# A graph-network kernel: its prologue rewritten in groups of two tiles, the lowest bf16 part made through PSUM

## The chip, the core and the metric

One core of one Trainium2 chip runs the whole program. The time is the device time of one execution in microseconds (us); of several executions the median is given. A profiled execution gives in addition a record of each instruction, from which the views in this document are taken. The engines are called TensorE (PE), VectorE (DVE), ScalarE (ACT), GpSimd (POOL) and SyncE (SP); SP here only issues DMAs.

## The reference

```python
h = jnp.maximum(_layernorm(x, axis=-1), 0.0)      # x: (6250, 256) f32
deg = segment_sum(ones, edge_dst)                 # 100000 edges, dst sorted
h = sage_mean(h, ...)      # h @ W1_self + mean of h over in-edges @ W1_neigh + b1
h = sage_pool(h, ...)      # relu(h @ W2_pool + b2_pool), max over in-edges, two products
h = sage_gcn(h, ...)       # (sum over in-edges + h) / (deg + 1) @ W3_neigh + b3
h = sage_mean(h, ...)      # W4_self, W4_neigh, b4
out = x + (h @ W_fc + b_fc)
```

Each edge adds row `h[src]` into node `dst`. The destinations crowd at the low nodes (they are 6250 times the square of a uniform number), so the first node tiles have very many edges and the last have few.

## The kernel before

The 6250 nodes are 49 tiles of 128. Precision is kept by writing each f32 value as a sum of three bf16 parts (`hi`, `mid`, `lo`), which TensorE multiplies with 0/1 or count matrices exactly and adds up in PSUM.

**Prologue (L648 to L967).** It makes three things. First, the table of layer 1: x is loaded tile by tile, normalized, put through relu, split into the three parts in the SBUF tensor `Z1`, and stored to `tab_h` in DRAM. `layer_norm` (L684) does five tiles at a time: per tile `bn_stats` and `bn_aggr` on VectorE, then for the group a square root (ScalarE), a reciprocal and a bias (VectorE), five relu activations (ScalarE), the cast `hi` (ScalarE, L701), the subtraction of `hi` (VectorE, L702), the cast `mid` (GpSimd, L703), the subtraction that gives `lo` (VectorE, L704) and one store of five tiles (SP, L705). x has three buffers of five tiles; group g + 3 is loaded behind group g. Second, the edge lists are put in place: `dst` and `src` are transposed by TensorE (`turn`, L856), the first edge of each window of nodes is found (`begins`, `begin_nodes`, `row_begins`), windows of edges are gathered by GpSimd and transposed (`window_rows`, L818), and keys are made of them (`window_keys`, `tail_keys`). `tail_keys` also makes the 0/1 table `M` (L894) and three checks of the input (L872, L901, L912), whose results are only read at the end of the kernel. Third, products of the weights (`product`) are made, one step per group.

Beside these the prologue begins the first count matrix: `made` (L646) is a list of 139 matrix steps for node block 0, each of which makes two one-hot tiles (`hs` by two ScalarE instructions or one on VectorE, L326 to L333; `hm` on VectorE, L335) and multiplies them (L341). `made.advance(part0)` does 62 of the 139 here (45 per cent).

**Layer 1 (L970 to L1032).** Node blocks 8 and up get their rows by gathers: GpSimd issues 474 indirect DMAs of 128 rows each (L478), one-hot tiles of the keys are made on VectorE (L474), TensorE adds the three parts (L500), VectorE adds the sums into `acc` with `M` (L529). The ring of gathered rows holds 14. The eight low blocks are dense products of count matrices with `Z1` (L559). All matrix steps that are left, and the dense products, form the hub, which is spread evenly over the gathers (L507), except for the last 24. Per gather one step of each "aside" generator is taken as well; `segments` (L591) is the only one. It loads `src` and `dst` once more, in blocks, for layer 2.

The order of the instructions on each engine is not that of the code. A planner lays them out by its own costs; a DMA with `keep_in_program_order`, and an engine inside `manual_schedule`, keep the order of the code. An instruction waits on its engine's queue in order, and everything behind it waits too, DMA issues on SP, ScalarE and GpSimd among them. DMAs of SP and ScalarE take eight completion semaphores in turn; one that takes a semaphore waits until the DMA that had it before has landed.

Of the kernel before, what the change touches and what calls it, by code (L numbers as in the profile page):

```python
# [27 lines left out]
PART0 = 45  # L28
# [50 lines left out]
def fast_path(  # L79
# [511 lines left out]
    def segments():  # L591
# [3 lines left out]
        for b, tb in enumerate(BLOCKS):  # L595
            t0 = offs[b] // P
            for flat, put in ((sflat, srcI), (dflat, dstI)):
                nc.sync.dma_start(
                    put[:, t0 : t0 + tb],
                    flat[offs[b] : offs[b + 1]].rearrange("(p t) -> p t", t=tb),  # L600
                )
# [43 lines left out]
    part0 = sum(k_of[:WT]) * PART0 // 100  # L645
    made = Hub(build(0, As[0], (sk1, mk1, 0), bpool, psb1, part0))  # L646

    with ExitStack() as pro:  # L648
        pst = pro.enter_context(tc.tile_pool(name="pst0", bufs=3, space=PSUM))
        psm = pro.enter_context(tc.tile_pool(name="psm0", bufs=3, space=PSUM))  # L650
        ep = pro.enter_context(tc.tile_pool(name="turn", bufs=1))


        dstI = scratch(T, I32)
        nc.sync.dma_start(dstI, dflat[0:EP].rearrange("(p t) -> p t", t=T))
# [6 lines left out]


        lp = pro.enter_context(tc.tile_pool(name="fln", bufs=2))
        xts = []
        groups = [(i0, min(5, NT - i0)) for i0 in range(0, NT, 5)]

        def load_x(g):
            i0, n = groups[g]
            xt = lp.tile([P, 5, FI], F32, name="xt", bufs=3)[:, :n, :]  # L670
            nf = min(n, NFULL - i0)
            if nf < n:
                nc.vector.memset(xt[(NREM // 32) * 32 :, nf, :], 0.0)
                nc.sync.dma_start(xt[:NREM, nf, :], x[NFULL * P : N, :])
            nc.sync.dma_start(
                xt[:, :nf, :],
                x[i0 * P : (i0 + nf) * P, :].rearrange("(c p) f -> p c f", p=P),
            )
            xts.append(xt)

        for g in range(3):
            load_x(g)

        def layer_norm(g):  # L684
            i0, LG = groups[g]
            xt = xts[g]
            mv = lp.tile([P, 5, 2], F32, name="mv")[:, :LG, :]
            for c in range(LG):
                st = lp.tile([P, 6], F32, name="st", bufs=4)
                nc.vector.bn_stats(st, xt[:, c, :])  # L690
                nc.vector.bn_aggr(mv[:, c, :], st)
            sd, rs, nb = (lp.tile([P, 5], F32, name=v)[:, :LG] for v in ("sd", "rs", "nb"))
            nc.vector.tensor_scalar(sd, mv[:, :, 1], EPS, None, op0=ALU.add)
            nc.scalar.activation(sd, sd, AF.Sqrt)
            nc.vector.reciprocal(rs, sd)
# [4 lines left out]
            hi, mid, lo = (Z1[:, i0 : i0 + LG, i * FI : (i + 1) * FI] for i in range(3))  # L700
            nc.scalar.copy(hi, xt)  # L701
            nc.vector.tensor_sub(xt, xt, hi)  # L702
            nc.gpsimd.tensor_copy(mid, xt)  # L703
            nc.vector.tensor_sub(lo, xt, mid)  # L704
# [25 lines left out]
        select(0)  # L730


# [9 lines left out]
        dlast = ep.tile([P, 1], F32, name="dlastf")  # L742
        nc.vector.tensor_copy(dlast, dstI[:, T - 1 : T])
        under = ep.tile([P, NC * P], BF16, name="under")
        nc.vector.tensor_scalar(under, iota_n, dlast, None, op0=ALU.is_gt)
        pc = bank(psm, "pm", "pc_c", (NC,))
        for c in range(NC):
            nc.tensor.matmul(pc[:, c : c + 1], under[:, c * P : (c + 1) * P], ones_b,
                             start=True, stop=True)
        cF = ep.tile([P, NC], F32, name="cF")  # L750
        nc.vector.tensor_scalar(cF, pc, float(P - 1), None, op0=ALU.min)
        cI = ep.tile([P, NC], I32, name="cI")
        nc.vector.tensor_copy(cI, cF)
# [5 lines left out]
        def begins(c):  # L759
            if c in (1, 2):  # L760
                row = As[0].rearrange("p s n -> p (s n)").bitcast(I32)[:, (c - 1) * T : c * T]
            else:
                row = ep.tile([P, T], I32, name="drow", bufs=1)
# [17 lines left out]
        def row_begins(b0, b1, cs):  # L781
            pa = bank(psm, "pm", "pa", (RB, 2))
            for b in range(b0, b1):
                for c in cs:
# [3 lines left out]
                                 start=False, stop=True)  # L788
            nc.vector.tensor_copy(atF[:, b0:b1, :], pa[:, b0:b1, :])
# [28 lines left out]
        def window_rows(b):  # L818
            mk = mk1 if b < RB1 // P else mkR
            got = []  # L820
            for flat in (dflat, sflat):
                t = ep.tile([P, P], I32, name="wrow", bufs=4)
# [4 lines left out]
                got.append(t)  # L827
            f = ep.tile([P, 2, P], F32, name="wrowf", bufs=2)
# [3 lines left out]
            for i in range(2):  # L832
                nc.tensor.transpose(pt[:, i, :], f[:, i, :], ident)
            r = b * P if b < RB1 // P else b * P - RB1
# [21 lines left out]
        def turn():  # L856
            for r, put in ((rD[:, JC:, :], dT), (rS, srcT)):
                for c0 in range(0, JR - JC, 4):
                    n = min(4, JR - JC - c0)
                    rF = ep.tile([P, 4, P], F32, name="rF", bufs=2)  # L860
                    nc.vector.tensor_copy(rF[:, :n, :], r[:, c0 : c0 + n, :])
                    pt = bank(pst, "pt", "pt_e", (4, P))
                    for c in range(n):
                        nc.tensor.transpose(pt[:, c, :], rF[:, c, :], ident)
                    nc.vector.tensor_copy(
                        put[:, c0 * P : (c0 + n) * P],
                        pt[:, :n, :].rearrange("p a b -> p (a b)"),
                    )
# [1332 lines left out]
```

## Time and profile before

| | us |
|---|---|
| median of 3 runs | 2768.62 (2766.17 to 2773.96) |
| the profiled execution | 2777.43 |
| its span, first to last instruction | 2775.6 |
| prologue, up to the first gather of layer 1 | 130.5 |
| layer 1, up to the last product of its gathers | 134.0 to 747.4 |

The profile's lines name the source line, the engine, the operation and the tiles (output `<-` inputs). A time in brackets behind an instruction is the idle time ahead of it, with what ended it. In a table of stages each engine has its busy time and, in brackets, its count of instructions. The profile follows one execution, and times of it are compared only with that execution's own.

### The profile page before, as it was taken

Reading aid. Unit: us, or ns where it says so; the run is one execution under the profiler, and the core shown is the slowest. Engines: PE = TensorE matmul, PEld = TensorE weight load, DVE = VectorE, ACT = ScalarE, POOL = GpSimd, SP = SyncE. Lnnn points to the kernel's source line nnn. Section 1 sums busy time; section 2 is a strip of 40 time slices with the busy share of each in tenths; the row PEclk is TensorE's granted clock in tenths of the full one; section 3 lists DMA queues with packets and bytes.
Section 4 is the critical chain, followed back from the end, with each engine's and each line's share of the span. In section 5 each row is a group of like instructions: output and inputs, shape, how many; then the busy total and the mean of one; then the engine's idle time right before and its main releaser. Section 6 shows DMA issues by size and latency. Waiting matters only on the chain.

```text
span 2775.6 us, 39285 instructions
## 1 busy us (share of the span) xinstructions
PE 2382.4 (86%) x11671; PEld 1280.7 (46%) x11671; DVE 2074.6 (75%) x5484; ACT 912.3 (33%) x2202; POOL 1940.8 (70%) x2260
## 2 busy tenths in 40 slices
PE   4379999999978566798899978985999999999998
PEld 2136666666544222343344433442444444565554
DVE  7978676766489889889899997871667776466655
ACT  3668676764268778421311121110000011000000
POOL 4277777777467777777777777754777776677775
PEclk9589999999989687899999988998999999999999
DMA  6556777777699999999999999977999998888886
GB/s 207 175 151 193 207 209 209 220 230 226 182 342 362 330 350 356 353 360 344 335 353 356 355 356 332 339 271 279 378 378 385 382 371 321 262 242 241 238 243 198
DMA packets 350539, 806.43 MB, mean 291 GB/s; under 512 B 55806, under 2 KB 147430, under 8 KB 350284
## 3 DMA queue, kind: packets, MB, share of 16 engines
q0 software_dynamic: 146160, 514.05, 56.6%
q1 hardware_dynamic: 137576, 207.04, 20.5%
q10 hardware_dynamic: 66580, 82.73, 8.9%
q8 instruction: 94, 1.54, 0.2%
q14 instruction: 129, 1.06, 0.1%
HBM read 605.25 MB, written 199.17 MB: 290 GB/s over the span
## 4 chain that ended last, share of the span: by engine, by line
PE 51%; DMA 27%; DVE 11%; issue 5%; POOL 3%; ACT 1%; SPq 0%; DVEq 0%; POOLq 0%; ACTq 0%
PE pd L559 14%; DMA X<-rows,srcIf 11%; PE pg L500 11%; PE pd L551 5%; DMA ring<-tab_h,srcT 4%; DVE run L1342 3%; DMA ring<-tab_s,srcE 3%; PE pm_hp L1010 3%; PE pm_hp L1013 3%; PE pm_prf L1269 3%; DMA rows<-X 3%; PE pd L552 2%; DVE X L1342 2%; POOL X L1361 2%; PE pg L495 2%
## 5 line engine op out<-in xcount | busy, mean ns | idle before, releaser
L1361 POOL DMA_INDIRECT X<-rows,srcIf x782 | 744.6, 952 | 281.4 <-issue 144.5
L1342 DVE SCALAR_TENSOR_TENSOR run<-run,samef,X 128x512 f32<-128x512 f32 x758 | 571.3, 754 | 52.5 <-DMA X<-rows,srcIf 48.4
L500 PE MATMUL pg<-ring,hot 128*128 128x259 bf16 (+1 forms) x2448 | 514.0, 321 | 59.7 <-DMA ring<-tab_h,srcT 34.6
L478 POOL DMA_INDIRECT ring<-tab_h,srcT x474 | 456.3, 963 | 152.2 <-issue 54.0
L529 DVE SCALAR_TENSOR_TENSOR acc<-pg,M,acc 128x256 f32<-128x256 f32 (+2 forms) x694 | 357.0, 539 | 107.6 <-PE pg L500 80.5
L478 POOL DMA_INDIRECT ring<-tab_r,srcE x342 | 334.1, 977 | 130.3 <-issue 56.9
L559 PE MATMUL pd<-r,ae 128*128 128x512 bf16 x1536 | 373.5, 384 | 35.4 <-DVE acc L1127 35.3
L478 POOL DMA_INDIRECT ring<-tab_s,srcE x314 | 300.1, 956 | 114.5 <-PE pg L496 36.2
L500 PEld LDWEIGHTS <-hot 128*128 128x128 bf16 x2448 | 240.3, 99 | 274.5 <-issue 113.3
L1342 DVE SCALAR_TENSOR_TENSOR X<-X,samef,run 128x512 f32<-128x512 f32 x379 | 281.6, 743 | 41.3 <-DVE hm L369 8.6
L551 PE MATMUL pd<-zt,ac 128*128 128x512 bf16 x882 | 305.0, 380 | 5.6 <-DMA ac<-tab_a 4.0
L559 PEld LDWEIGHTS <-ae 128*128 128x128 fp8e4 x1536 | 151.3, 99 | 251.9 <-issue 106.5
L474 DVE TENSOR_SCALAR hot<-iota_bf,keyE 128x128 bf16<-128x128 bf16 x656 | 160.3, 268 | 108.6 <-PE pg L500 78.3
L552 PE MATMUL pd<-zt,ac 128*128 128x256 bf16 x882 | 241.0, 273 | 0.2 <-DVE zt L307 0.2
L559 PE MATMUL pd<-zt,ac 128*128 128x512 bf16 x816 | 224.7, 380 | 0.0
L1269 PE MATMUL pm_prf<-unf,hTf 128*128 128x512 f32 x392 | 189.9, 612 | 4.6 <-ACT hTf L1259 4.6
L341 PE MATMUL pb<-hm,hs 128*128 128x392 bf16 x461 | 150.9, 349 | 48.6 <-DVE hm L335 43.0
L333 ACT ACTIVATE hs<-ht,onef 128x128 bf16<-128x128 bf16 x423 | 161.7, 393 | 85.5 <-PE pb L341 84.5
L559 PE MATMUL pd<-Z,A 128*128 128x256 bf16 (+1 forms) x1176 | 185.6, 273 | 0.4 <-ACT A L346 0.2
L474 DVE TENSOR_SCALAR hot<-iota_bf,keyT 128x128 bf16<-128x128 bf16 x474 | 122.8, 270 | 61.2 <-PE pg L500 59.2
L335 DVE TENSOR_SCALAR hm<-iota_w,mk 128x392 bf16<-128x392 f16 x461 | 151.6, 339 | 17.3 <-PE pb L341 16.3
L332 ACT ACTIVATE ht<-iota_bf,sk 128x128 bf16<-128x128 bf16 x423 | 159.0, 396 | 7.0
(342 smaller groups left out, 3457.6 us busy)
## 6 DMA issues: line engine op xcount, KB each, us to landing
rows<-X SPq DMA_DIRECT2D x385, 256.0 KB
tab_r<-r ACTq DMA_DIRECT2D x49, 384.0 KB
tab_t<-th SPq DMA_DIRECT2D x49, 256.0 KB
rows<-hpf SPq DMA_DIRECT2D x49, 256.0 KB
th<-tab_t ACTq DMA_DIRECT2D x49, 256.0 KB
X<-rows,srcIf POOLq DMA_INDIRECT x782
ac<-tab_a ACTq DMA_DIRECT2D x90, 112.0 KB
tab_h<-Z SPq DMA_DIRECT2D x9, 965.0 KB
```

Source lines behind the costliest of these rows:

```text
L332: nc.scalar.activation(t, iota_b, AF.Abs, bias=sk[:, r : r + 1])
L333: nc.scalar.activation(hots[0], t, AF.Relu, bias=one, scale=-1.0)
L474: nc.vector.tensor_scalar(hot[j], iota_b, keyT[:, j - jb : j - jb + 1], None, op0=ALU.is_equal)
L478: nc.gpsimd.indirect_dma_start(out=ring[:, j % deep, :], out_offset=None, in_=table, in_offset=bass.IndirectOffsetOnAxis(ap=srcT[:, j - jb ...
L500: nc.tensor.matmul(pg[:, : F + c], hot[j], X[:, part * F : (part + 1) * F + c], start=(k == 0 and part == 2), stop=(k == n - 1 and part == 1),
L529: nc.vector.scalar_tensor_tensor(acc[d], half, m, acc[d], op0=ALU.mult, op1=ALU.add)
L551: nc.tensor.matmul(hold[0], a, z[:, : 2 * F], start=(s == ss[0]), stop=False)
L552: nc.tensor.matmul(hold[0][:, :F], a, z[:, 2 * F :], start=False, stop=(s == ss[-1]))
L559: nc.tensor.matmul(hold[0][:, : F + c], a, z[:, part * F : (part + 1) * F + c], start=(s == ss[0] and part == 2 and s != own), stop=(s == ...
L1269: nc.tensor.matmul(pm, hT[:, c, :], un[:, c, :], start=False, stop=(c == KH - 1))
L1342: nc.vector.scalar_tensor_tensor(put, held, st, row, op0=ALU.mult, op1=ALU.max)
L1361: nc.gpsimd.indirect_dma_start(out=X[:, k, :], out_offset=None, in_=tab_p, in_offset=bass.IndirectOffsetOnAxis(ap=srcI[:, t : t + 1], axis=0),
```

## The change

- Groups have two tiles instead of five (25 groups); x has seven buffers of two tiles instead of three of five. `layer_norm` is cut into pieces, `stats`, `inverse`, `scaled`, `middle` and `lowest`, and the pieces of neighbouring groups are interleaved: in iteration g come the reciprocal of g + 1, the statistics of g + 2 with the relus and the cast of g + 1 among them, the closing of g - 1, the load of g + 6 and the subtraction of g. VectorE keeps this order (`manual_schedule`).
- The lowest part is no longer subtracted on VectorE. TensorE multiplies the rest by the identity into PSUM (f32) and adds the middle part times minus the identity (bf16); ScalarE copies the difference from PSUM as bf16.
- All other work of the prologue (`extras`) is laid in pieces behind the subtractions of the groups 2, 6, 8, 10, 13, 15, 17 and all from 18 on, with a piece that needs another engine's answer one or more groups behind the piece that asked. The first statistics come before any of it.
- The three checks of the input go to layer 1 as the first aside generator (`tail_checks`), ahead of `segments`; the loads of `segments` keep their place in the code instead of being drawn into the start of the prologue.
- `part0` is 10 instead of 62: ten matrix steps of block 0 are done in the prologue and 129 left to the hub.
- Gathers of windows have eight buffers instead of four; rows for `begins` are put into tensors that exist already.

```diff
-PART0 = 45
...
-    part0 = sum(k_of[:WT]) * PART0 // 100
+    part0 = 10
...
-        groups = [(i0, min(5, NT - i0)) for i0 in range(0, NT, 5)]
+        groups = [(i0, min(2, NT - i0)) for i0 in range(0, NT, 2)]
...
-            xt = lp.tile([P, 5, FI], F32, name="xt", bufs=3)[:, :n, :]
+            xt = lp.tile([P, 2, FI], F32, name="xt", bufs=7)[:, :n, :]
...
-            nc.scalar.copy(hi, xt)
-            nc.vector.tensor_sub(xt, xt, hi)
-            nc.gpsimd.tensor_copy(mid, xt)
-            nc.vector.tensor_sub(lo, xt, mid)
+        def middle(g):
+            i0, LG = groups[g]
+            nc.vector.tensor_sub(xts[g], xts[g], Z1[:, i0 : i0 + LG, :FI])
+            nc.gpsimd.tensor_copy(Z1[:, i0 : i0 + LG, FI : 2 * FI], xts[g])
+            pl = lows[g] = bank(psl, "pl", "pl", (2, FI))[:, :LG, :]
+            nc.tensor.matmul(pl, ident, xts[g], start=True, stop=False)
+
+        def lowest(g):
+            i0, LG = groups[g]
+            pl = lows.pop(g)
+            nc.tensor.matmul(pl, minus_b, Z1[:, i0 : i0 + LG, FI : 2 * FI], start=False, stop=True)
+            nc.scalar.copy(Z1[:, i0 : i0 + LG, 2 * FI : 3 * FI], pl)
             nc.sync.dma_start(
                 tab_h[i0 * P : (i0 + LG) * P, :].rearrange("(c p) f -> p c f", p=P),
                 Z1[:, i0 : i0 + LG, :],
...
+        with tc.manual_schedule(engines={mybir.EngineType.DVE}):
+            stats(0)
+            select(0)
+            inverse(0)
+            stats(1, lambda: scaled(0))
+            chunks_at()
+            for c in range(NC):
+                begins(c)
+            for g in range(len(groups)):
+                if g + 1 < len(groups):
+                    inverse(g + 1)
+                if g + 2 < len(groups):
+                    stats(g + 2, lambda: scaled(g + 1), lambda: lowest(g - 1) if g else None)
+                else:
+                    if g + 1 < len(groups):
+                        scaled(g + 1)
+                    lowest(g - 1)
+                if g + 7 - 1 < len(groups) and g:
+                    load_x(g + 7 - 1)
+                middle(g)
+                next(steps, None)
+                if g in (2, 6, 8, 10, 13, 15, 17):
+                    extras((2, 6, 8, 10, 13, 15, 17).index(g))
+                elif g > 17:
+                    extras(g - 17 + 6)
+            lowest(len(groups) - 1)
+            for _ in steps:
+                pass
+            tail_keys()
...
-             aside=[segments()])
+             aside=[tail_checks(wk), segments()])
```

In `extras` the parts from group 6 on are those of the old code, in this order: the first node rows and the first halves of the transposed lists (2, 6), the window gathers of the first block, eight in a row (8), the other node rows (10), the transposed windows (13, 15, 17) and the keys of block 0 (17), then the narrower windows with `check_room` (18, 21) and the tile numbers (23), with one or two of the ten matrix steps in each of the groups 18 to 24.

More of the change, by code (lines that the diff above doesn't have):

```diff
@@ L685, in layer_norm, with inverse, scaled @@
+        def inverse(g):
+            mv, sd = norms.pop(g)
+            rs = lp.tile([P, 2], F32, name="rs", bufs=3)[:, : groups[g][1]]
+            nc.vector.reciprocal(rs, sd)
+            norms[g] = mv, rs
+        def scaled(g):
             i0, LG = groups[g]
             xt = xts[g]
[L687 to L691, printed above, removed]
@@ L762, in begins @@
             else:
-                row = ep.tile([P, T], I32, name="drow", bufs=1)
+                row = same.bitcast(I32) if c else srcI
             nc.gpsimd.indirect_dma_start(
```

261 lines of the change are left out of this document (163 added, 98 removed).

## The prediction

> **What bounds it now.** I read the span in stages first. The columns are busy time and instruction count of each engine, the granted TensorE clock, the DMA share and rate.
>
> ```profile
> core 0: us, PE busy (x) PEld busy (x) DVE busy (x) ACT busy (x) POOL busy (x), PEclk, DMA share, GB/s
> 8.00:50.00 42.00, 16.62 (x65) 12.58 (x66) 29.40 (x96) 12.39 (x25) 22.52 (x55) 1.00 0.66 205
> 50.00:125.00 75.00, 30.72 (x94) 12.87 (x92) 70.73 (x225) 47.72 (x109) 14.84 (x71) 0.67 0.61 192
> 125.00:130.50 5.50, 2.78 (x8) 1.15 (x9) 5.50 (x15) 5.02 (x18) 2.98 (x106) 0.50 0.42 147
> 130.50:225.00 94.50, 71.21 (x372) 39.22 (x371) 77.83 (x341) 67.08 (x209) 70.42 (x70) 0.87 0.59 162
> 225.00:450.00 225.00, 204.46 (x1405) 142.94 (x1404) 159.17 (x610) 155.32 (x425) 170.63 (x179) 0.99 0.72 205
> 450.00:700.00 250.00, 248.94 (x1696) 174.67 (x1694) 173.50 (x648) 153.83 (x394) 189.64 (x199) 1.00 0.75 220
> ```
>
> The prologue is VectorE's: 70.73 of 75 us busy from 50 to 125. Before 50 VectorE idles 12.6 of 42 us. The rest of layer 1 has two masters: GpSimd issues one gather per 225/179 = 1.257 us, and from 450 TensorE is full too (248.94 of 250). The first stretch is worse: 70 gathers in 94.5 us, where 70 x 1.257 = 88 would do, so 6.5 us are lost there. From layer 2 on the instruction order of the changed program is the same on every engine; the whole change is therefore the move of the end of layer 1.
>
> Where the prologue ends is read from GpSimd's timeline: the last middle part, the 164 memsets of `lim`, then a wait for the last stored rows, then the first gather.
>
> ```profile
> 122.21 1.07 POOL L703 CAST Z<-xt 128x1024 bf16<-128x1024 f32 x1 [3.64 <-DVE xt L702]
> 123.23 4.75 POOL L967 MEMSET lim<- 1x1 f32 x164
> 130.52 1.03 POOL L478 DMA_INDIRECT ring<-tab_h,srcT  x1 [2.54 <-PE pb L341]
> ```
>
> **Start of the new prologue.** Two rows say why the old one starts late: VectorE waits 3.85 us for the shifted copy of dst, and ScalarE issues the first weight loads at 22.97.
>
> ```profile
> 18.26 1.09 DVE L872 TENSOR_TENSOR wrongf<-X,X 128x896 bf16<-128x896 int32 x1 [3.85 <-DMA X<-dflat]
> ```
> ```profile
> 22.97 0.84 ACTq L261 DMA_DIRECT2D wl<-in_L_gnn_W_self  x2
> 28.20 2.56 ACT L698 ACTIVATE xt<-xt,nb,rs 128x256 f32<-128x256 f32 x5 [13.64 <-DVE nb L696]
> 30.67 0.19 ACT L694 ACTIVATE sd<-sd 128x5 f32<-128x5 f32 x1
> 30.79 1.26 ACT L701 CAST Z<-xt 128x1280 bf16<-128x1280 f32 x1
> ...
> 46.71 0.59 ACT L266 COPY wT<-pt_w 128x512 f32<-128x512 f32 x1 [3.01 <-PE pt_w L265]
> ```
>
> In the changed program the first weight load stands on ScalarE's queue ahead of the first normalization and shares a completion semaphore with that copy of dst, which is there at 18.26; the second stands behind the first normalization. So ScalarE cannot begin before about 18.5, and 0.8 of issue, two tiles of 2.56/5 = 0.51, a square root and a cast of 1.26 x 2/5 = 0.50 put group 0's subtraction, the first of all, at about 21.5. The old first cast ends at 32.05; the new one, at 20.8, is some 11 us ahead, since the statistics no longer queue on VectorE with the work on dst.
>
> **VectorE's work after that.** Groups of VectorE's instructions, 0 to 130.5 (count | busy us, mean ns | idle before):
>
> ```profile
> L690 DVE BATCH_NORM_STATS2 st<-xt 128x6 f32<-128x256 f32 x49 | 18.8, 399 | 0.8 <-DMA xt<-in_x 0.8
> L702 DVE TENSOR_TENSOR xt<-xt,Z 128x1280 f32<-128x1280 f32 (+1 forms) x10 | 14.6, 1459 | 0.8 <-ACT Z L701 0.8
> L704 DVE TENSOR_TENSOR Z<-xt,Z 128x1280 bf16<-128x1280 f32 (+1 forms) x10 | 14.5, 1448 | 0.0
> L335 DVE TENSOR_SCALAR hm<-iota_w,mk 128x392 bf16<-128x392 f16 x34 | 13.5, 440 | 0.0
> ...
> L894 DVE TENSOR_SCALAR M<-tile_of 128x6 f32<-128x6 f32 (+6 forms) x41 | 4.0, 167 | 0.0
> ...
> L693 DVE TENSOR_SCALAR sd<-mv 128x5 f32<-128x5 f32 (+1 forms) x10 | 1.7, 168 | 0.0
> L912 DVE SCALAR_TENSOR_TENSOR wrongf<-wrongf,X 128x640 bf16<-128x640 bf16 x1 | 1.6, 1610 | 0.0
> L901 DVE TENSOR_TENSOR wrongf<-X,dB 128x128 bf16<-128x128 f32 x5 | 1.3, 278 | 0.0
> ...
> L844 DVE TENSOR_TENSOR mk<-mk,sk 128x512 f32<-128x512 f32 x1 | 0.7, 679 | 0.0
> ```
>
> From 8 to 130.5 VectorE is busy 29.4 + 70.7 + 5.5 = 105.6 us. Out go the lowest part, 14.5; the checks L872, L901, L912, 4.0, with their reduction of about L872's length, 1.1 (an estimate); 24 of 34 one-hots at 0.440, 10.6; and `M`, 4.0, which now stands behind the last subtraction. In come 24.5 subtractions of 0.679 for 14.6, +2.0, and three small instructions in 25 groups instead of 10, 15 x 3 x 0.168 = 7.6. That leaves 81; about 5 are done before 21.5 (three groups' statistics, 6 x 0.399, one selection, small ones) and 4 are keys behind the last subtraction: **72 us** after 21.5.
>
> **ScalarE beside it.** A group's loop, when the square root is queued last: reciprocal 0.17, statistics 0.40, bias 0.17, two tiles 1.02, lowest copy from PSUM 0.59 (L266's row), cast 0.50, root 0.19, in all 3.0; with the root first 2.0. The order has both. VectorE's own loop is about 2.3 by single durations, 1.9 as they overlap. In the 11 iterations with no side work I charge 0.8 each: 9 us (bounds 0 and 2.0 each). In the other 14 the side work covers it.
>
> **GpSimd in between.** Eight window gathers in a row, then four, stand ahead of the next group's middle cast; TensorE's closing product, ScalarE's copy, and in order behind it casts and roots wait for that.
>
> ```profile
> 29.50 0.95 POOL L823 DMA_INDIRECT wrow<-dflat,atI  x1 [0.30 <-issue]
> ```
>
> At 1.25 each the eight take 10 us, while VectorE has some 8 us of its own until it needs the next root, and the copies behind add 2.5: 4.5 us lost; the four cost 2.5. Together 7 (0 to 13).
>
> **TensorE's new product** is not a term while the clock is up: two records of 0.59 for a 512-wide f32 product, and a bf16 one of less, are under 2 of some 3.5 us a group.
>
> ```profile
> L277 PE MATMUL pm_b<-w2pf,b1c 128*128 128x512 f32 x8 | 3.6, 592 | 0.0
> ```
>
> The last subtraction ends near 21.5 + 72 + 9 + 7 = 109.5; a small cast and then the 4.75 of `lim`, now not hidden behind a store of four tiles, give the first gather at about 115.5, against 130.5: **15 us earlier**. DMA is no term: its share was 0.61 of 75 us with the same bytes, and six groups are loaded ahead.
>
> **Back in layer 1.** 52 matrix steps of the first block move behind the first gather on paper (62 to 10); in the two TensorE orders, by gather 30 there are 62 steps before and 60 after, by gather 60 155 and 117, by gather 240 321 and 308. So the early stretch gets no more TensorE work, but VectorE gets the checks there (5.1) and starts late: the `lim` memsets hold it, as this row of the chain shows (a 0.28 instruction took 2.87), then keys and `M` follow before the first one-hot.
>
> ```profile
> 125.24 2.87 DVE hm L335
> ```
>
> I put the early loss at 4 (0 to 10) instead of 6.5: -2.5. From gather 240 TensorE has 13 steps and 36 dense products more:
>
> ```profile
> L341 PE MATMUL pb<-hm,hs 128*128 128x392 bf16 x461 | 150.9, 349 | 48.6 <-DVE hm L335 43.0
> ...
> L559 PE MATMUL pd<-Z,A 128*128 128x256 bf16 (+1 forms) x1176 | 185.6, 273 | 0.4 <-ACT A L346 0.2
> ```
>
> 13 x 0.33 + 36 x 185.6/1176 = 10 us on a full engine; the 20.5 us that TensorE idles from 225 to 450 take some of it, so 5 (0 to 10). Net -15 - 2.5 + 5 = **-12.5**, rounded to -12: 2765 for the profiled execution of 2777.4 us (span 2775.6), which lies 8.8 above the median of the runs; 2757 for the median.
>
> **Rivals.**
> *VectorE alone paces* (ScalarE and gathers cost nothing): first gather 16 earlier still by 9 + 7, early loss gone, late term 10: -15 - 16 - 6.5 + 10 = -27, 2741. For it: each side step was laid one or more groups behind its source; against: casts and roots share one in-order queue.
> *The gain is given back in layer 1*: early loss 10, late term 10, and the two stalls at 13 not 7: -15 + 6 + 3.5 + 10 = +4; with half of it -4. Middle: 2769, no change. For it: 248.94 of 250.
> *Slower:* TensorE at half clock (0.67 and 0.50 are granted from 50 to 130) takes 2.4 for the f32 product and closes late; with the closing copy ahead of cast and root on ScalarE, 2.4 + 0.43 + 0.59 + 0.50 + 0.19 + 0.17 make a loop of 4.3, with hand-overs 4.5. Eleven iterations at 4.5 instead of 2.7 are 20, eight lightly loaded others by 1.0 each 8: -12 + 28 = +16, 2785. It eats up the gain from about 3.7 us an iteration (11 x 1.0 + 8 x 0.2 = 12.6).
> *Transfers pace:* a 256 KB store lands in 2.00.
>
> ```profile
> 758.05 2.00 DMA rows<-hpf
> ```
>
> Twenty-five loads of 2 and stores of 3 one after the other would be 125 us and put the first gather near 140: +12, 2781. Against it: several are in flight, and load and store of a group do not wait for each other. The Trainium skill, "DMA: Bandwidth & Descriptors", section "Anatomy of one DMA", gives about 2.0 us fixed per transfer plus bytes over 436 GB/s and advises few large ones, which speaks against groups of two; by its figures a pair would be an estimated 5.5 us, also only if nothing overlaps.
>
> **Chances.** Forecast 0.46, VectorE alone 0.17, given back 0.24, half clock 0.08, transfers 0.05. A measurement of this kernel tells 0.3%, 8.3 us, from no change. Faster: 0.17 + 0.38 of the forecast = 0.55; within: 0.24 + 0.08 of the forecast + 0.01 = 0.33; slower 0.12, the rest of the last two. The likeliest case alone spans 2749 to 2765, its stalls at 0 and 13. The range reaches from 2741 to 2776.
>
> **What would show it.** Right: first subtraction at 21 to 23, first gather at 112 to 119, VectorE 85% busy between, 70 gathers in under 94 us, TensorE full from before 450. Wrong: the first gather after 125 with ScalarE waiting on TensorE (half clock) or VectorE on x (transfers), or a first gather on time and layer 1 as much longer.

## The result and the profile after

The changed kernel takes **2780.42 us** (median of 7 runs, 2776.78 to 2784.39) against 2769.09 (median of 7, 2766.17 to 2773.96) for the kernel before: ratio **1.0039, 95% interval 1.0027 to 1.0050**, slower by 0.4 per cent, clear of the noise. Predicted were 2757, between 2741 and 2776, and faster. The two profiled executions differ by 3.0 us only (2780.42 and 2777.43), because that of before lay 8.3 above its median; the prediction's own measure, the end of layer 1, moved by +9.6 (issue of the last gather).

Stages of the changed kernel, in the columns of the table of before:

```profile
core 0: us, PE busy (x) PEld busy (x) DVE busy (x) ACT busy (x) POOL busy (x), PEclk, DMA share, GB/s
8.00:50.00 42.00, 26.57 (x76) 12.78 (x77) 24.25 (x97) 25.25 (x55) 13.14 (x38) 1.00 0.76 244
50.00:125.00 75.00, 49.23 (x140) 23.57 (x139) 53.19 (x197) 42.55 (x104) 23.57 (x41) 0.72 0.48 152
125.00:133.22 8.22, 3.58 (x10) 1.50 (x10) 8.15 (x15) 4.12 (x12) 5.30 (x166) 0.71 0.36 125
133.22:225.00 91.78, 64.46 (x343) 36.11 (x342) 80.42 (x365) 50.45 (x136) 70.68 (x70) 0.86 0.62 171
225.00:450.00 225.00, 201.91 (x1401) 141.20 (x1401) 167.71 (x687) 163.26 (x457) 170.55 (x179) 1.00 0.71 206
450.00:700.00 250.00, 249.89 (x1690) 174.83 (x1689) 174.96 (x642) 161.47 (x416) 184.87 (x195) 0.99 0.73 216
```

VectorE lost its work (53.19 of 75 us, before 70.73) and the prologue got no shorter: it waits instead. In layer 1 the rows look like those of before, but GpSimd issues 195 gathers between 450 and 700, not 199, with TensorE full. The end of the prologue on GpSimd, to be held against the three rows of before:

```profile
126.51 0.40 POOL L724 CAST Z<-xt 128x256 bf16<-128x256 f32 x1 [2.28 <-DVE xt L723]
126.85 4.96 POOL L1082 MEMSET lim<- 1x1 f32 x164
133.22 1.30 POOL L477 DMA_INDIRECT ring<-tab_h,srcT  x1 [1.40 <-issue]
```

The first gather comes at 133.22, forecast 115.5, before 130.52. What VectorE, then ScalarE, waited for between the first subtraction and the last (us in total, times, longest):

```profile
DVE rs L707 <- ACT sd L701: 18.5, 12, 4.7
DVE crow L282 <- ACT crow L278: 4.8, 1, 4.8
DVE xt L723 <- ACT Z L719: 2.7, 2, 1.6
DVE wrowf L864 <- PE pt_r L868: 1.6, 1, 1.6
```
```profile
ACT Z L732 <- PE pl L731: 19.9, 13, 4.8
```

VectorE waits for square roots; ScalarE, which makes them, waits for the closing products of TensorE, though not before 53.5 us: all of the 19.9 lie behind that. No row names a load of x.

The way through layer 1 is told by when a gather is issued, counted from 0 (us, from GpSimd's timelines; at its own pace of 1.257 GpSimd needs 91.8 for the 73 gathers from 400 on):

| kernel | first | 70 | 400 | last | 400 to last |
|---|---|---|---|---|---|
| before | 130.5 | 225.1 | 641.3 | 735.5 | 94.2 |
| changed | 133.2 | 225.2 | 640.7 | 745.1 | 104.4 |

The late start is made up by gather 70. All of the loss arises in the last 73 gathers.

The same prologue does not end at the same time in every execution. In e7 and e14, whose prologue is that of the kernel before, the first gather comes at 129.8 and 128.5; in e6 and e9, with that of the changed kernel, at 131.7 and 132.7. A difference of under 2 us between two first gathers is therefore not read as an effect.

The second and the fifth set of experiments (e5 to e8, e17, e18) ran under a condition in which every gather took about 1.5 us instead of 1.26 and every kernel, the one before too, 3267 to 3323 us; of them I use the prologue alone, compared within the set.

### The profile page after: what moved, and what is told of

It is laid out like the page before. It is cut to its first block, busy times and chain, and to the rows that moved or that the text cites. A ratio compares the mean times of both kernels' runs of the same rounds, so it can differ in the third digit from the quotient of the medians.

```text
span 2778.6 us, 39559 instructions
## 1 busy us (share of the span) xinstructions
PE 2411.8 (87%) x11746; PEld 1292.8 (47%) x11746; DVE 2071.4 (75%) x5570; ACT 918.9 (33%) x2205; POOL 1937.8 (70%) x2275
## 4 chain that ended last, share of the span: by engine, by line
PE 36%; DMA 24%; DVE 8%; issue 4%; POOL 3%; ACT 1%; ACTq 0%; POOLq 0%; DVEq 0%; SPq 0%
DMA X<-rows,srcIf 12%; PE pd L558 11%; PE pg L499 7%; PE pd L550 5%; DVE run L1457 4%; DMA ring<-tab_s,srcE 3%; DMA rows<-X 3%; PE pd L551 2%; DVE X L1457 2%; PE pm_prf L1384 2%; POOL X L1476 2%; PE pg L494 2%; DMA zt<-tab_r 2%; DMA ring<-tab_r,srcE 1%; PE pm_w L268 1%
## 5 line engine op out<-in xcount | busy, mean ns | idle before, releaser
L332 ACT ACTIVATE hs<-ht,onef 128x128 bf16<-128x128 bf16 x397 | 154.3, 393 | 114.7 <-PE pb L340 113.9
L331 ACT ACTIVATE ht<-iota_bf,sk 128x128 bf16<-128x128 bf16 x397 | 152.9, 397 | 11.4 <-DVE sk L889 3.2
```

What stands on the lines that cost most here:

```text
L331: nc.scalar.activation(t, iota_b, AF.Abs, bias=sk[:, r : r + 1])
L332: nc.scalar.activation(hots[0], t, AF.Relu, bias=one, scale=-1.0)
```

## The experiments

Ratios are to the kernel before, run beside each kernel, with 95% intervals. "Waits" are VectorE's.

An edit can move three things: when VectorE's first subtraction comes, how long it is from the first to the last of the 25 (the stage), and how long from the start of the last to the first gather. In us:

| run | first subtraction | stage | VectorE idle in it | last subtraction to first gather |
|---|---|---|---|---|
| changed | 21.1 | 105.0 | 30.5 | 7.2 |
| e1 | 20.8 | 97.3 | 22.4 | 6.9 |
| e2 | 20.7 | 110.0 | 22.7 | 6.6 |
| e10, e11 | 14.6, 14.7 | 96.7, 96.6 | 22.5, 21.9 | 12.3, 12.4 |
| e13 | 13.9 | 91.6 | 16.6 | 12.7 |
| e15 | 14.8 | 99.5 | 12.8 | 6.7 |
| e16 | 15.0 | 83.5 | 7.3 | 13.1 |
| e17, e18 | 13.8, 13.8 | 84.6, 93.0 | 8.0, 4.7 | 10.1, 10.9 |

**e1: without the weight products.** The prologue also makes `Wa`, `Wb` and `crow` from five products of TensorE.

```diff
-            yield from product(ep, pst, psm, W1_self, w2p, Wa)
-            yield from product(ep, pst, psm, W1_neigh, w2p, Wb)
-            yield from bias_rows(psm, b1c, w2p, crow, b2p)
+            for w, put in ((W1_self, Wa), (W1_neigh, Wb)):
+                nc.scalar.dma_start(put, w.rearrange("(k p) f -> p k f", p=P))
+            nc.vector.tensor_copy(crow, b2p)
+            yield
```

> Changed kernel; the weight products of the prologue (pm_w, pt_w, pm_b and their ScalarE copies) are left out, Wa, Wb and crow are filled with the plain rows instead. Theory Q (TensorE's in-order queue paces the new prologue: from 21 to 53.5 us it is busy 29.8 of 32.4, 22.7 of it weight products that stand ahead of the closing products of the lowest part; ScalarE's closing copy waits, and casts and roots behind it): the nine first groups take 3.0 us each instead of 4.1, first gather at about 123 instead of 133.2, and about 9 us of the total gone (2771). Rival S (the loop VectorE, ScalarE, GpSimd, TensorE of one group paces by its own hand-overs, whatever else TensorE does): first gather after 131, total within 3 us of the changed kernel (2778 to 2781).

Measured: first gather 125.0, last 734.3; ratio 0.9994 (0.9980 to 1.0008). Theory Q has the size, 8.2 of the 9 us, and S falls. What suggested Q is TensorE's part of the stage in the changed kernel, and its timeline there:

```profile
21.00:53.50 32.50, 29.81 (x81) 14.20 (x82) 20.33 (x78) 22.64 (x52) 7.86 (x12) 1.00 0.56 185
```
```profile
25.73 4.94 PE L268 MATMUL pm_w<-w2pf,wT 128*128 128x512 f32 x8
30.51 0.38 PE L731 MATMUL pl<-Z,minus_b 128*128 128x512 bf16 x1
30.73 1.02 PE L726 MATMUL pl<-xt,identf 128*128 128x512 f32 x2
...
45.71 3.70 PE L268 MATMUL pm_w<-w2pf,wT 128*128 128x512 f32 x8 [0.54 <-ACT wT L265]
49.24 3.60 PE L276 MATMUL pm_b<-w2pf,b1c 128*128 128x512 f32 x8
52.68 0.38 PE L731 MATMUL pl<-Z,minus_b 128*128 128x512 bf16 x1
```

TensorE is busy 29.81 of 32.50 us, and four of the six closing products (L731) come behind a weight product of 3.6 to 4.9.

But the gain does not lie where Q has it. The first nine groups take 3.2 us each without the products and 3.4 with them (3.0 and 4.1 were expected). 6.4 of the 8.2 lie between the ninth and the tenth subtraction. There VectorE of the changed kernel adds up the bias row `crow` and copies `pa`, and waits for TensorE at both:

```profile
53.49 0.69 DVE L282 TENSOR_TENSOR crow<-crow,b2pf 128x512 f32<-128x512 f32 x1 [4.82 <-ACT crow L278]
55.43 0.17 DVE L820 COPY atF<-pa 128x8 f32<-128x8 f32 x1 [1.24 <-PE pa L815]
```

Without the weight products TensorE also ran more of the new f32 products slowly. Each is a pair of records, 1.02 us in the rows above; 7 of the 10 pairs up to 53.5 us took 1.5 to 2.1 us, in the changed kernel one of 7. This may have eaten up part of the relief in the first nine groups; no run separates it.

**e2: the lowest part on VectorE again.**

```diff
-            nc.tensor.matmul(pl, minus_b, Z1[:, i0 : i0 + LG, FI : 2 * FI], start=False, stop=True)
-            nc.scalar.copy(Z1[:, i0 : i0 + LG, 2 * FI : 3 * FI], pl)
+            nc.vector.tensor_sub(Z1[:, i0 : i0 + LG, 2 * FI : 3 * FI], xts[g], Z1[:, i0 : i0 + LG, FI : 2 * FI])
```

> Changed kernel; only the lowest part is again subtracted on VectorE (25 subtractions of 0.69 = 17 us), TensorE's two products and ScalarE's closing copy are gone. Q: VectorE's idle time between the first and the last subtraction falls from 30 us to about 12 (gathers and bias row stay), so first gather at about 132 and the total about 1 lower (2779). S: the root still goes VectorE to ScalarE and back in every group, idle time stays above 22, first gather at about 142, total about 8 higher (2788).

Measured: first gather 137.3, last 746.0; ratio 1.0031 (1.0015 to 1.0046). Half way between the two in the first gather, 17 us of subtraction for 4.1; VectorE's idle time, 22.7, is as S had it. Roots still cost 5.4 of waits, the middle casts behind the window gathers 8.6. The bias row costs 5.8 here too, although TensorE has no new product and is busy only 22.0 of the 32.5 us up to 53.5 (it stood 7.0 us for VectorE ahead of the fourth weight product): that wait does not need the new products.

**e3: kernel before with 10 matrix steps in the prologue.**

```diff
-    part0 = sum(k_of[:WT]) * PART0 // 100
+    part0 = 10
```

> Kernel before; only the number of matrix steps in the prologue is 10 instead of 62. VectorE loses 24 one-hots of 0.44 in the prologue, so the first gather comes some 9 us earlier (121). Theory L (the 52 steps cost 10 us on a full TensorE from gather 240 on, whole): the end of layer 1 moves by about 0 to +2 (2769 to 2771). Rival (the hub absorbs them in TensorE's idle time; the changed kernel's layer 1 ended late only because it began late): end 9 earlier, 2760.

Measured: first gather 133.0, gather 400 at 638.4, last 740.8; ratio 1.0017 (1.0002 to 1.0033). The first gather came later, against both theories: the planner drew the same one-hots into the prologue all the same (34 of L335 in both), and moved 12 of the `hs` from ScalarE to VectorE, 2.9 us. But by gather 70 TensorE had made 129 steps, before 157, and from gather 400 on it took 102.4 against 94.2: the moved steps alone cost 8.2 us at the end. Theory L holds, its rival falls.

**e4: the memsets of `lim` early.** `limits(d)` is the old loop body.

```diff
                 next(steps, None)
+                for d in range(H1 + 6 * (g - 1), min(H1 + 6 * g, NT)):
+                    if g:
+                        limits(d)
```

> Changed kernel; only the 164 memsets of lim are moved from behind the last group into the groups 1 to 7, where GpSimd idles 2 to 3 us a group. First gather 5 us earlier (128) by all theories. If an earlier first gather reaches the end of layer 1 (L: from gather 60 to 400 GpSimd paces): total 4 to 5 lower (2776). If the first 60 gathers are bound by TensorE and VectorE, which begin the count matrix only when the keys are there: 0 to 2 lower (2779).

Measured: first gather 133.0, last 746.0; ratio 1.0031 (1.0017 to 1.0045). The first gather did not move, which no theory had expected. GpSimd now stands idle where the memsets were:

```profile
126.68 0.40 POOL L724 CAST Z<-xt 128x256 bf16<-128x256 f32 x1 [2.28 <-DVE xt L723]
133.02 0.96 POOL L477 DMA_INDIRECT ring<-tab_h,srcT  x1 [5.94 <-DMA stash_e<-keyT]
```

The closing of the last group and the last stores (issued at 128.89 and 130.42) take as long; of the two stores the wait is put down to the later, which of them it was is open.

**e5: closing one group later.**

```diff
-                    stats(g + 2, lambda: scaled(g + 1), lambda: lowest(g - 1) if g else None)
+                    stats(g + 2, lambda: scaled(g + 1), lambda: lowest(g - 2) if g > 1 else None)
```

> Changed kernel; only the closing of the lowest part (TensorE's product with the middle part, ScalarE's copy, the store) comes one group later, in iteration g for g - 2. In the changed kernel ScalarE waits 19.9 us for closing products, and VectorE 18.5 us for the roots behind them. Theory Q (it is the place of the copy in ScalarE's queue, ahead of cast and root): these waits fall to under 10 us, the first gather comes 6 to 10 us earlier (123 to 127), the total 6 to 10 lower. Rival T (TensorE and GpSimd pace by their mere work, the wait only moves to another instruction): first gather within 2 us of 133, total unchanged.

Measured: first gather 130.7, against 131.7 for the same prologue in e6 of the same set (ratio 0.9958, 0.9941 to 0.9974). The waits for roots did fall, from 18.5 to 9.0, but those for casts rose from 2.7 to 7.6 and the bias row's stayed (4.3). The first gather is as rival T has it: TensorE is still busy 29.68 of 32.5 us up to 53.5.

**e6, e7 and again e9, e14: the hub bent to the front.**

```diff
-                    hub.advance(before + math.ceil((len(hub.work) - before) * (at - wait)
-                                                   / (T - j0 - wait - rest)))
+                    u = min(1.0, (at - wait) / (T - j0 - wait - rest))
+                    hub.advance(before + math.ceil((len(hub.work) - before) * (u + 0.15 * u * (1 - u))))
```

> Changed kernel; only the spread of the hub over the gathers of layer 1 is bent: at the share u of the gathers u + 0.15 u (1 - u) of the steps are done instead of u. Theory L (TensorE idles 23 us between gathers 70 and 250, because the steps are counted out evenly, and is full afterwards, so that the 52 moved steps cost 10 us at the end): last gather at about 735 instead of 745, total 9 to 10 lower (2771). Rival (the end is late because the prologue is): no change; or VectorE, 92 per cent busy up to gather 60, cannot make the one-hots earlier: the early gathers fall 5 us behind and stay so.

> Kernel before, with the same bent spread of the hub: the control to the run on the changed kernel. L: here TensorE costs the last 74 gathers only 1 to 4 us beyond 1.257 us each (641.3 to 735.5 instead of 734.3), so last gather 1 to 4 us earlier, total 0 to 4 lower (2766 to 2769).

Here every gather took 1.5 us, so that GpSimd bounds all of layer 1 (ratios 0.9947, 0.9925 to 0.9968, and 1.0018, 0.9992 to 1.0044): the two tell nothing of the end. e9 and e14 are the same kernels with gathers of 1.26.

> The same kernel as e6 (changed kernel, hub bent by 0.15), since in the set of e6 every gather of both kernels took 1.5 us and layer 1 was bound by the gathers throughout, so that it could not tell the theories apart. Where a gather takes 1.26 us: theory L as for e6, last gather at about 735, total 9 to 10 lower than the changed kernel, level with the kernel before (2769 to 2772). Rival: no change (2780).

> The same kernel as e7 (kernel before, hub bent), for a set in which a gather takes 1.26 us. L: last gather 1 to 4 us earlier than 735.5, total 0.9985 to 1.000 of the kernel before. If the bend alone made e11 better than the kernel before: last gather at 727, ratio 0.997.

Measured, changed kernel: first gather 132.7, last 732.3; ratio 0.9994 (0.9983 to 1.0005). Kernel before: 128.5 and 734.1; 0.9990 (0.9977 to 1.0002). Theory L: the same bend takes 12.8 us off the changed kernel's last gather and 1.5 off the other. TensorE's idle time before 450 is where they come from (201.91 in the changed kernel):

```profile
225.00:450.00 225.00, 211.07 (x1461) 148.62 (x1459) 173.54 (x698) 169.91 (x477) 170.62 (x179) 0.99 0.72 207
```

**e8: weight products spread.**

```diff
-                next(steps, None)
+                if g in (0, 3, 6, 9) or g > 11:
+                    next(steps, None)
```

> Changed kernel; the four weight products and the bias row are begun behind the groups 0, 3, 6, 9 and 12 instead of 0, 1, 2, 3 and 4, and the sum of crow on VectorE stands behind group 16 instead of 8. Q: leaving them out altogether brought the first gather 8.2 us earlier; spread, TensorE has 3 groups of 1.4 and one product of 4.5 in 9 us, so 4 to 6 of the 8.2 us come back (first gather at 127 to 129), and VectorE's wait of 4.8 for the bias row is gone. Rival (half clock: where the products are thinner, TensorE runs the closing products at half rate and loses what was won): first gather at 131 to 133.

Measured: first gather 129.9, 1.7 earlier than in e6, no more than two executions of one prologue differ by (ratio 0.9950, 0.9926 to 0.9974). Less than expected: the bias row's wait went, but 7.8 us for the node rows' product (`pa`), now behind a weight product, took its place.

**e10: weight products in layer 1; e11: and the hub bent.**

```diff
-             aside=[tail_checks(wk), segments()])
+             aside=[products1(), tail_checks(wk), segments()], front=0.15)
```

(e10 without `front`; `products1`, its loads and its tiles move to layer 1's pool.)

> Changed kernel; the weight products and the bias row, 22.7 us of TensorE's work, are made in layer 1 beside the first gathers (TensorE idles 27 us before 225) instead of in the prologue. Theory Q (TensorE, busy 29.8 of 32.4 us up to 53.5, held the prologue there): first gather at about 125, as when they were left out, and as they now lie in idle time the last gather about as there, 734 to 738; total 8 to 11 lower than the changed kernel (2770). Rival (the products only move and cost the same 8 us in layer 1, where the tail of node tiles waits for them): first gather at 125, last gather at 743 or later.

> The two edits together: products in layer 1, hub bent by 0.15. Q and L: the gains add, last gather at about 728 (125 + 474 x 1.257 = 721 and some loss in the first 60), total 17 to 20 lower than the changed kernel and 6 to 9 lower than the kernel before (2761). Rival: TensorE has no idle time left before gather 250, so the bend brings nothing beside the moved products (2770).

Measured, e10: first gather 123.6, last 734.8, ratio 1.0001 (0.9989 to 1.0012). Of the 10.4 us at the last gather 6.3 are there at gather 400. The 9.6 at the first gather are a sum of three: the first subtraction comes 6.4 earlier, since no load of weights or bias stands on ScalarE's queue ahead of the first normalization any more; the stage is 8.3 shorter; and the way from the last subtraction to the first gather is 5.1 longer, since the last store of the table now stands behind that of the keys (issued at 120.08, the last subtraction at 111.3). e11: 123.6 and 726.6, **0.9967 (0.9954 to 0.9979)**: the two edits bring 18.5 us at the last gather, alone 10.4 and 12.8, and the kernel is faster than before.

**e12: the window gathers two by two.** Behind each of the groups 8 to 11 one pair instead of eight behind 8.

> As e11, and the eight gathers of windows issued two each behind the groups 8 to 11 instead of eight behind group 8. GpSimd then holds the middle cast for 2.5 us a group instead of once for 10; TensorE's wait of 4.6 and VectorE's of 4.7 us at 66 are to go: first gather 3 to 4 us earlier than in e11 (121 to 122), total 3 lower than e11. Rival (the four small waits add up to the large one): the same as e11.

Measured: 124.3 and 725.7, ratio 0.9968 (0.9955 to 0.9981). Tells nothing: GpSimd's order is the planner's, and it issued the eight in a row as before.

**e13: e11 with the closing one group later (edit of e5).**

> As e11 (products in layer 1, hub bent), and the closing of the lowest part one group later. In e11 ScalarE still waits some 22 us for closing products and VectorE 16 us for the roots behind them, with TensorE busy only 65 of 106 us. Theory Q, second half (the closing copy stands ahead of cast and root in ScalarE's queue; in e5 this could not show because TensorE was full up to 54): these waits fall below 8 us, first gather 6 to 10 us earlier than in e11 (114 to 118), total 5 to 9 lower than e11 (0.994 of the kernel before). Rival T (TensorE at half clock and the gathers on GpSimd take this time by their mere work): first gather 121 to 124, total as e11.

Measured: first gather 118.2, 5.4 earlier than e11, 5.0 of it in the stage; last 721.7; ratio 0.9957 (0.9940 to 0.9973). Theory Q's second half, a little under its low end. The waits of e11 and of e13:

```profile
DVE rs L707 <- ACT sd L701: 16.0, 11, 4.7
```
```profile
DVE xt L723 <- ACT Z L719: 7.3, 3, 3.5
DVE rs L707 <- ACT sd L701: 3.6, 4, 1.8
```

The roots come on time now; part of the wait has moved to the cast.

**e15: e11 with the lowest part on VectorE (edit of e2).**

> As e11, with the lowest part subtracted on VectorE instead of made by TensorE and copied by ScalarE. Takes 17 us of VectorE's time in, and gives up TensorE's and ScalarE's parts. If the way through PSUM pays once TensorE is free: first gather 4 to 10 us later than in e11 (128 to 134), total 4 to 8 higher than e11. If the waits that it brings eat up what it saves: first gather within 3 of e11.

Measured: first gather 121.0, last 726.2; ratio 0.9959 (0.9947 to 0.9971). The first gather is 2.6 us earlier than in e11, and so the way through PSUM looks slower than the subtraction it replaced. But the stage is 2.9 longer here (99.5 against 96.6). What is shorter, by 5.7, is the way to the first gather: here the last store of the table stands ahead of that of the keys. In the stage the way through PSUM is the faster one, by 2.9 here and by 5.0 between the changed kernel and e2, far less than the 17 us of subtraction.

**e16: e13 with GpSimd held to the code's order and the window gathers in pairs.**

```diff
-            nc.gpsimd.tensor_copy(Z1[:, i0 : i0 + LG, FI : 2 * FI], xts[g])
+            tc.keep_in_program_order(nc.gpsimd.tensor_copy(Z1[:, i0 : i0 + LG, FI : 2 * FI], xts[g]))
...
+                if g - 8 in range(1, W1):
+                    window_gathers(g - 8)
```

> As e13, and GpSimd kept in the order of the code for the middle casts and the gathers of windows, two of these behind each of the groups 8 to 11 (in e12 the planner still issued the eight in a row). Q: the wait of 4.7 us behind the eight gathers falls to under 1, first gather 2 to 4 us earlier than in e13, total 1 to 3 lower. Rival: the gathers end later and the keys, on which the one-hots of block 0 wait, come later by as much: no gain.

Measured: first gather 111.6, last 715.5; ratio **0.9934 (0.9916 to 0.9952)**, the best of all. The gain over e13 is more than the 2 to 4 expected; the edit also holds the middle casts to the code's order, and the two are not separated. Between the first subtraction and the last VectorE idles 7.3 of 83.5 us, in the changed kernel 30.5 of 105:

```profile
15.03:98.53 83.50, 56.33 (x149) 22.62 (x150) 76.17 (x278) 58.53 (x143) 33.45 (x54) 0.80 0.64 207
```

**e17: and the stores in the code's order; e18: e17 with the lowest part on VectorE.** In e16 the last store of the table stood behind that of the keys, though its copy had ended at 101.27:

```profile
106.85 0.33 SPq L950 DMA_DIRECT2D stash_e<-keyT  x1
107.28 0.37 SPq L733 DMA_DIRECT2D tab_h<-Z  x1
```

> As e16, and the stores of the table and of the keys kept in the order of the code on SyncE. In e16 the last store of the table was issued at 107.28 although its last copy ended at 101.27, because the store of the keys stood ahead of it, and the first gather (111.6) waited for it. Expected: store at 101.7, first gather at about 106, and if an earlier first gather reaches the end (as in e10 to e16) the last gather about 5 earlier, total 0.991 to 0.992 of the kernel before. Rival (the loads of the weights, issued from 100.45 on, hold the store back in the DMA engines): first gather after 109.

> As e17, with the lowest part subtracted on VectorE (x loaded one group later, as its buffer is read one group longer). In e16 VectorE was busy 96 of 106 us, so with the obstacles gone VectorE paces and the 17 us that the way through PSUM takes off it should now count: first gather 10 to 15 us later than in e17, total 0.4 to 0.5 per cent higher. Rival (as between e11 and e15, where the way through PSUM was no faster: what it saves on VectorE it costs in waits): first gather within 4 us of e17.

Measured: first gather 108.5 and 117.7 (ratios 0.9965, 0.9934 to 0.9996, and 0.9987, 0.9960 to 1.0015). The store was issued at 100.58, and still the gather came 7.9 later; what held it is open (the DMA engines were all busy from 100 to 106, and the profile puts the last 4.26 us down to a weight load, of which the rival spoke). The way through PSUM now counts more: 9.2 us at the first gather, 8.3 in the stage, a little under the 10 to 15 expected.

## Why the prediction was wrong

**Start of the prologue: right.** The first subtraction stands at 21.06, forecast 21.5, and e10, where the weight loads are gone from there, bears out the reason: 14.6. First and last of VectorE's 25 subtractions, then the stage between them:

```profile
21.06 0.69 DVE L723 TENSOR_TENSOR xt<-xt,Z 128x512 f32<-128x512 f32 x1 [1.11 <-ACT Z L719]
...
126.03 0.42 DVE L723 TENSOR_TENSOR xt<-xt,Z 128x256 f32<-128x256 f32 x1
```
```profile
21.06:126.03 104.97, 76.56 (x212) 36.36 (x213) 74.47 (x278) 64.96 (x153) 31.37 (x53) 0.80 0.51 166
```

**VectorE's work: right.** 74.5 us busy from there to the last subtraction (21.06 to 126.03), forecast 72.

**Its waits: wrong, 30.5 us instead of 16.** The step that failed is "TensorE's new product is not a term while the clock is up ... under 2 of some 3.5 us a group". I held the new products against the length of a group, not against what TensorE already had to do there, and the weight products have no term in my sum at all. They are still begun one per group, but a group has two tiles now instead of five. So up to 53.5 us TensorE makes all five with their transposes, 16.0 + 3.6 + 3.1 = 22.7 us, and the new products fill what is left:

```profile
L268 PE MATMUL pm_w<-w2pf,wT 128*128 128x512 f32 x32 | 16.0, 648 | 0.5 <-ACT wT L265 0.5
L276 PE MATMUL pm_b<-w2pf,b1c 128*128 128x512 f32 x8 | 3.6, 592 | 0.0
L264 PE MATMUL pt_w<-identf,wl 128*128 128x128 f32 x16 | 3.1, 315 | 5.0 <-DMA wl<-in_L_gnn_W_self 5.0
```

In the old prologue VectorE did not wait for them (its sum of the bias row is at 79.2 and waits for nothing). In the new one they cost the stage 7.7 to 8.4 us: so much shorter it is without them (e1, e10, e11). Most of it VectorE waits itself, 4.8 for the bias row, whose product ends this work, and 1.2 for `pa` behind it, although both were laid one or more groups behind their source. e2 has the first of these waits without any new product, so it is the weight products in their new place that cost this, more than the new products beside them. That each group's closing product queues behind a weight product, ScalarE's copy behind that, and cast and root behind the copy, is seen in the timeline but is worth little of this: the first nine groups became 1.1 us shorter in e1 and 1.9 in e11, if slower products did not hide more. Spreading or deferring within the same stage brought 1 to 2, not clear of the scatter (e5, e8).

That last chain costs later in the prologue: ScalarE waits there 19.9 us for closing products, with cast and root behind. This is the term "ScalarE beside it ... 9 us", which was not too small: with TensorE relieved, the copy's place in ScalarE's queue is worth 5.0 in the stage (e13). The waits for roots, 18.5, are near the 16 forecast for ScalarE and GpSimd together; the excess is the bias row (4.8), transposes and `pa` on TensorE (3.5) and casts (2.7) for the most part.

**Window gathers: right in size.** 4.5 us for the eight in a row were forecast; the chain shows 4.6 on TensorE, 4.8 on ScalarE, 4.7 on VectorE:

```profile
66.52 0.59 PE L731 MATMUL pl<-Z,minus_b 128*128 128x512 bf16 x1 [4.61 <-POOL Z L724]
66.89 1.91 PE L726 MATMUL pl<-xt,identf 128*128 128x512 f32 x2
...
73.10 2.08 PE L726 MATMUL pl<-xt,identf 128*128 128x512 f32 x2
```

With GpSimd's order mended they go; the stage of e16 is 8.1 shorter than that of e13. So 8.4 (e11), 5.0 (e13) and 8.1 (e16) make up the 21.5 us by which the stage shrinks from 105.0 to 83.5; e5 shows the second worth little before the first was gone. That the first gather moves by as much, from 133.2 to 111.6, is chance: a start 6 us earlier and an end 6 us longer cancel.

**The memsets: wrong cause, near size.** "The 4.75 of `lim`, now not hidden" is refuted by e4. The last closing and store take the same time: 6.8 from the end of the last subtraction (126.45) to the first gather, forecast 6.0.

**Early layer 1: right in size, not shown in its reason.** -2.5 was forecast; the lag of +2.7 at the first gather is +0.1 at gather 70. But the forecast was for a start 15 us earlier, and of the runs that did start earlier than the kernel before, that stretch gained 0.1 in e10 and 1.8 in e11 and lost 1.1 in e16 (each with the weight products in it).

**Late layer 1: wrong by half.** The forecast was +5 of 10, since "the 20.5 us that TensorE idles from 225 to 450 take some of it". It took none: the steps are counted out by gather, so TensorE idles before gather 250 whatever waits behind. At gather 400 it had 6 steps and 27 dense products more to do than in the kernel before, in e3 6 and 26. The full upper bound came, 104.4 - 94.2 = 10.2; e3 puts 8.2 of it on the moved steps, e9 gets all of it back. The other 2 are open; with as many steps moved, e1, e2 and e10 need 100.3 to 100.9 for these gathers, so that the term is 6 to 10 by the execution.

**The sum:** -15 became +2.7, -2.5 held, +5 became +10: +9.6 where -12.5 stood (0.7 was gained in between). One more thing follows: the prologue's lag of 2.7 was nothing by gather 70, but leads of 7 to 19 us over the kernel before went through to gather 400 nearly whole (e10: -6.9 at both; e16: -18.9 and -17.5).

**The rivals.** *Half clock* has nearly the right time (2785, chance 0.08) and the sign it gave, ScalarE waiting on TensorE, but not the cause, so the time is luck. Up to 53.5 us the pairs of the f32 product took 1.02, but for the first (1.92), and TensorE was simply full. After 60 us 10 of the 15 full pairs took about 2.0, as in the rows above, and the bf16 product then 0.59 to 0.63 (0.43 in that rival's sum, which no row shows). The Trainium skill, "TensorE: Matmul & The Clock Gate", section "HAM oscillation — how this bites in real kernels", has the array fall to half rate after an idle gap of about 3.4 us; the 4.61 ahead of 66.52 agrees. Not every slow pair has such a gap: that at 86.41 took 2.00, and the longest gap shortly ahead of it was 1.66. What the slow pairs cost no run separates; e16 has 12 of them to the changed kernel's 11, and idles 7.3 us. *Transfers pace* is out: no wait of VectorE in the changed kernel between its first and its last subtraction is for x, and e16 loads and stores the same pairs by 111.6; the fit quoted in that rival is one for transfers that GpSimd issues, and SP issues these. *VectorE alone paces* is what e16 comes near in the stage (83.5 us, of them 76 busy, where 72 were forecast), not at the first gather: 111.6, and 16 earlier than the forecast would be 99.5. *Given back in layer 1* was right in one of its three terms, the late one.

## What to carry to other kernels

When work moves to an idle engine, add it to what that engine's queue holds in that same stage, look for the places where the pacing engine itself needs a result of that queue, and look at what stands behind the hand-over on the next engine: a copy out of PSUM in an in-order queue delays all that is behind it. The busy time saved on the pacing engine is only an upper bound of the gain until every other queue in the loop has been checked, and the obstacles show one at a time. An experiment that moves work can shift the start and the end of a stage as well as its length; read the three apart. Work that is dealt out by a count fills no idle time by itself; moved into such a stage it costs its full price wherever the engine is full.

## What the runs showed of the hardware

The row of `lim` memsets holds up one VectorE instruction until the row ends (131.81): the same 128x640 operation takes 4.53 us beside them in the changed kernel and 0.48 in e4, where they are elsewhere. A one-hot that ran beside the row just before, at 127.41, took its usual 0.30.

```profile
127.64 4.53 DVE L938 TENSOR_SCALAR keyT<-keyT 128x640 int32<-128x640 int32 x1
```
```profile
127.75 0.48 DVE L938 TENSOR_SCALAR keyT<-keyT 128x640 int32<-128x640 int32 x1
```

The Trainium skill, "SBUF — State Buffer", section "Who interferes with whom", has the loser of the port pair wait for the other's whole instruction; here it waited for the rest of a row of 164.

The clock column can stand at 1.00 where products run slowly. From 23 to 30 us in the changed kernel it says 1.00, and the pair at 24.03 took 1.92 us, the next ones 1.02. In e15 TensorE is busy 12.63 of 59 us, the column says 1.00, and a product of 128x392 takes 503 ns, where 339 is the mean over the whole changed kernel:

```profile
60.00:119.00 59.00, 12.63 (x37) 5.37 (x37) 54.59 (x179) 29.89 (x76) 17.93 (x156) 1.00 0.47 146
```
```profile
L340 PE MATMUL pb<-hm,hs 128*128 128x392 bf16 x15 | 6.3, 503 | 17.9 <-DVE hm L334 17.8
```
```profile
L340 PE MATMUL pb<-hm,hs 128*128 128x392 bf16 x461 | 146.1, 339 | 11.2 <-DVE hm L334 10.8
```

The duration of a known product is the surer sign.
